# A pixel-transformer block on one core: the cross-attention stretch is planned anew (two join banks, half-step products with U, ternary weights in one step, a shared port in the plan)

## The chip, the core and the metric

The kernel runs on one core of a Trainium2 chip. The core has five engines with a queue of instructions each, which run in order: TensorE (PE, with its weight loads PEld), VectorE (DVE), ScalarE (ACT), GpSimd (POOL) and SyncE (SP), which here only issues DMAs. They meet through semaphores. The metric is the device time of one execution in microseconds, as the median of several runs.

## The reference

Two samples of 1024 tokens with 256 features go through a conditioned transformer block and then a quantised feed-forward layer, all in float32.

```python
h1 = adaln(x, t, norm1_w, norm1_b)              # layernorm(x) * (1 + scale) + shift
x = mha(h1, h1, attn1_wq, attn1_wk, attn1_wv, attn1_wo, attn1_bo) + x
h2 = adaln(x, t, norm2_w, norm2_b)
x = mha(h2, context, attn2_wq, attn2_wk, attn2_wv, attn2_wo, attn2_bo) + x
h3 = adaln(x, t, norm3_w, norm3_b)
x = glu_ff(h3, ff_w1, ff_b1, ff_w2, ff_b2) + x  # a * gelu(gate) @ w2 + b2
...
h = bitlinear(x, w1, b1)     # rmsnorm, rows rounded to 8 bits, weights to -1, 0, 1
h = jax.nn.gelu(h, approximate=False)
return bitlinear(h, w2, b2)
```

Attention has 16 heads of 64; the context has 77 keys for each sample. The ternary weights are `clip(round(w * scale), -1, 1) / scale` with `scale = 1 / mean(|w|)`.

## The kernel before, in words

**Three stretches.** The first runs self-attention in a loop written out by hand (up to about 770 us). The second, from there to about 961 us, is ordered by a planner and holds the end of self-attention, all of cross-attention and the preparation of the ternary weights. The third, also planned, is the gated feed-forward with the quantised layer behind it.

**The planner.** `Plan.add(engine, us, fn, after, rank, ring, behind)` records a step: its engine, how long it is taken to be, what it waits for, its rank among ready steps (a smaller number first), and a ring of PSUM banks that it takes a bank from. `Plan.run` plays the steps through with those durations, always takes the engine that can begin first, and calls each step's function then. That fixes the order of the instructions in the queues of PE, DVE, ACT and POOL. The durations do nothing on the chip. SP's order is made by the framework.

**Self-attention's end.** A unit `u` is a pair of heads with half of the tokens; `LAST` is number 31. Its scores (L425) of eight key blocks are copied by ACT (L1072), DVE keeps a running maximum `macc` (L441), which is folded (L446 to L463), goes through DRAM (`md`, `wide`, L467 and L468) and to a PSUM bank `mb` (L472). DVE subtracts it (L481; POOL for block 5, L477), ACT takes exponentials (L484), POOL adds them up in `pacc` (L491), PE multiplies with V (`pav`, L499, copied out at L515). The sums: PE adds over partitions (`tot`, L522, bank "f"), ACT copies (L532), SP packs them through DRAM (L536, L541), DVE inverts (L544), SP spreads them (`rinv`, L547 and L549), POOL normalises (L555). `back_to_tokens` then multiplies with the output weights in four steps t = 0, 2, 4, 6 (`po`, L360, all in bank "f"), and DVE adds each to the residual `r_sb` (L412), through a list `due` which `settle` empties.

**Cross-attention** works in four batches of 512 tokens. Keys and values are folded into G and U beforehand. For a batch, PE makes five tiles of scores against G (`sc`, L846, two banks in turn); ACT copies each to `p` (L856), DVE keeps the maximum (L862) and halves it (`largest`, L866). PE turns `macc` (a **join**, L873, four 128x128 transposes), DVE folds it to one maximum for each head and row and spreads it (`few`, `wide`, L877 and L883), PE turns it back, and DVE subtracts that row from each `p` (L896). ACT takes exponentials (L901 to L906), POOL sums them (L912, L916). The sums go the same way through PE, DVE (with a reciprocal, L881) and PE; POOL divides two of the tiles by them (L928, from a copy, L920), DVE three (L930). Then four products with U, of ten pieces each (`out`, L937, banks "av" and "f" in turn), which DVE adds to the residual (L949). The joins use two half banks, "A" and "B". Before, a batch's maximum is turned into B and back into A, its sums into A and back into B.

**Norms between.** `half_norm` takes statistics on DVE (L116, L117), begins a root there (L135, L84), steps it on POOL in 14 small instructions (L142 to L147), centres on ACT (L154), turns on PE (`pt_n`, L163) and scales on ACT (L170). It makes the second sample's input of cross-attention and the feed-forward's first input. POOL adds the output bias (L181).

**Ternary weights** w1 and w2, one after the other: SP loads them (`raw`, L1345), ACT takes sums of absolute values (L1363), PE the mean (`pm`, L1374), DVE scales, clips and rounds in two tiles of three operations (L1390, L1388, L1393), PE turns them (`pt_w`, L1407), ACT copies (L1411). Before, w2 is loaded into the tiles of w1 once those are free. `load_ff` loads the feed-forward's weights (L1331, L1333). The third stretch's products are L1799 and L1825.

Of the kernel before, what the change touches and what calls it, by code (L numbers as in the profile page):

```python
# [18 lines left out]
FP = mybir.dt.float32  # L19
# [24 lines left out]
def block_kernel(ctx: ExitStack, tc: tile.TileContext, a: dict, out: bass.AP):  # L44
# [141 lines left out]
    class Plan:  # L186
# [6 lines left out]
        def add(self, engine, us, fn, after=(), rank=0.0, ring=None, behind=()):  # L193

            behind = [s for s in behind if s is not None]
            after = [s for s in after if s is not None] + behind
            self.steps.append((engine, us, fn, after, rank, ring, behind))
            return len(self.steps) - 1  # L200

        def run(self, bufs):
# [6 lines left out]
            end, free = {}, dict.fromkeys(("PE", "ACT", "DVE", "POOL", "SP"), 0.0)  # L209
            left = set(range(len(self.steps)))  # L210

            def ready(s):
# [12 lines left out]
                return max([free[engine]] + [end[a] + l for a, l in zip(need, late)])  # L225

            while left:
# [19 lines left out]
                free[engine], end[s] = t + busy, t + made  # L247
                left.remove(s)
# [12 lines left out]
    with ExitStack() as sa:  # L261
# [137 lines left out]
        def back_to_tokens(b, grp, t):  # L399

            aT = aTs[b, grp]
            po = piece_bank("po")
# [431 lines left out]
        class Batch:  # L834


            def __init__(self, n):
                self.n, self.b, self.at = n, n // 2, n % 2 * 512
                self.sc, self.t = {}, {}
# [92 lines left out]
            def out(self, i, bank):  # L932
                self.po = getattr(self, "po", {})
                po = self.po[i] = bank
                for piece in range(NPIECE):
                    at = piece % 2 * 512 + i * P
                    nc.tensor.matmul(  # L937
                        po[:, :D],
# [5 lines left out]
                if i == 3:  # L944
                    del self.t
# [176 lines left out]
        settle()  # L1122
# [9 lines left out]
        row, sums, steps = {}, {}, {}  # L1132
# [44 lines left out]
        for u in (LAST - 2, LAST - 1, LAST):  # L1177
            s = add("PE", 0.75, lambda u=u: summed(u, piece_bank), [running.get(u)], -55, "f")
# [6 lines left out]
            )  # L1185
        given = []
        for t in range(0, TB, 2):
            u = LAST - 1 + t // 4
            s = add(
                "PE", 1.9, lambda t=t: back_to_tokens(B - 1, NP // 2 - 1, t),  # L1190
                [normal[u], normal[LAST - 2]] + given[-1:], -45 + t, "f",
            )
            given.append(add("DVE", 0.7, settle, [s], -45 + t))


        def half_norm(n, b, half, ready, rank, turn_after=()):
# [5 lines left out]
            s = add("DVE", 0.4, lambda: norm.root_begun(at, 4), s, rank)  # L1202
            s = add("POOL", 2.9, lambda: norm.root_stepped(at, 4), [s], rank)
# [51 lines left out]
        for n, x in enumerate(batches):  # L1255
            r = 10.0 * n
            b, half = n // 2, n % 2
            kept, larger = {}, {}
            for k in range(NTILE):
# [8 lines left out]
                score[n, k] = add("PE", 3.5, lambda x=x, k=k: x.scores(k), waits, r, "s", room)  # L1268
# [11 lines left out]
            s = add("DVE", 0.65, x.largest, [larger[NTILE - 1]], r - 21)  # L1280
# [630 lines left out]
```

## Time and profile before

| | us |
|---|---|
| median of 3 runs | 1180.77 (1179.68 to 1182.17) |
| the profiled execution | 1184.35 |
| its span on the core | 1181.7 |

| stretch, us | PE busy | DVE busy | ACT busy | POOL busy |
|---|---|---|---|---|
| 20 to 770 | 735.92 | 649.98 | 618.53 | 637.95 |
| 770 to 961 | 182.37 | 132.73 | 79.12 | 115.87 |
| 961 to 1181.7 | 211.96 | 144.85 | 109.24 | 84.72 |

The span runs from the first to the last instruction that the profiler recorded; 2.65 us of the profiled execution lie around it. In the rows below, an operation is named by its line, its engine, its output and inputs, its shape, and in brackets the idle time of the engine before it with what ended that. A matmul's end is modelled, so neighbours overlap by some tenths; distances between starts are exact. A float32 product is two records.

### The profile page before, as it was taken

What the parts mean: (1) busy time and instruction counts of PE and PEld (TensorE: products, weight loads), DVE (VectorE), ACT (ScalarE), POOL (GpSimd) and SP (SyncE); (2) the same over time, 40 slices, a digit from 0 to 9 for tenths busy, and PEclk for the clock granted to TensorE, in tenths of its full rate; (3) what the DMA queues carried; (4) which work ended last, traced back from release to release, by engine and by line L of the source; (5) the groups of instructions that cost most, each with busy time, mean ns of one, the idle gap of its engine ahead of it and who ended that gap; (6) DMA issues with size and microseconds to landing.
All of it is one profiled execution on the core that took longest, in us unless ns stands there. A gap on an engine that the chain in (4) does not pass through costs nothing.

```text
span 1181.7 us, 16400 instructions
## 1 busy us (share of the span) xinstructions
PE 1146.3 (97%) x5812; PEld 557.9 (47%) x5812; DVE 936.0 (79%) x1324; ACT 814.7 (69%) x1017; POOL 849.5 (72%) x644
## 2 busy tenths in 40 slices
PE   8998999999999999999999999999899999999997
PEld 4332334334334343343433333346577766486685
DVE  4799789879888988898978988966777733578597
ACT  4788887888887888888789878754633311556366
POOL 5589888888888788889878998877845613433235
PEclk9999999999999999999999999999999999999999
DMA  7111212212121221211113212121102021000000
GB/s 233 37 32 46 79 49 65 71 53 70 46 79 60 62 62 56 74 49 57 52 52 103 72 38 86 55 64 41 45 18 90 1 65 34 1 18 10 10 9 28
DMA packets 65031, 64.15 MB, mean 54 GB/s; under 512 B 23675, under 2 KB 54709, under 8 KB 64309
## 3 DMA queue, kind: packets, MB, share of 16 engines
q1 hardware_dynamic: 64885, 63.10, 17.2%
q8 instruction: 45, 0.74, 0.3%
q14 instruction: 37, 0.30, 0.1%
q10 hardware_dynamic: 64, 0.02, 0.0%
HBM read 55.36 MB, written 7.73 MB: 53 GB/s over the span
## 4 chain that ended last, share of the span: by engine, by line
PE 78%; DVE 14%; ACT 5%; issue 2%; DMA 1%; POOL 1%; SPq 0%; DVEq 0%; ACTq 0%; POOLq 0%
PE sc L425 17%; PE pav L499 16%; PE pp L360 8%; PE pu L1799 8%; PE sc L846 5%; PE pv L360 4%; PE po L1825 4%; DVE macc L441 4%; PE po L937 4%; DVE sT L481 3%; PE po L360 3%; ACT sT L1072 2%; PE tot L522 1%; PE pu L1654 1%; DVE p L896 1%
## 5 line engine op out<-in xcount | busy, mean ns | idle before, releaser
L491 POOL TENSOR_TENSOR pacc<-pacc,sT 128x1024 f32<-128x1024 f32 x192 | 455.6, 2373 | 47.2 <-ACT sT L484 36.7
L1072 ACT COPY sT<-sc 128x1024 f32<-128x1024 f32 x256 | 247.6, 1015 | 55.5 <-PE sc L425 48.8
L441 DVE TENSOR_TENSOR macc<-macc,sc 128x1024 f32<-128x1024 f32 x192 | 233.6, 1217 | 63.0 <-ACT sT L1072 51.7
L484 ACT ACTIVATE sT<-sT 128x1024 f32<-128x1024 f32 x256 | 259.2, 1061 | 11.7 <-DVE sT L481 10.8
L425 PE MATMUL sc<-qT,kT 64*128 64x512 f32 x1024 | 258.0, 619 | 6.4 <-DVE macc L441 5.8
L481 DVE TENSOR_TENSOR sT<-sT,mb 128x1024 f32<-128x1024 f32 x224 | 260.4, 1207 | 2.5 <-ACT mb L472 2.4
L499 PE MATMUL pav<-sT,v 128*64 128x512 f32 x1024 | 249.3, 607 | 4.8 <-ACT sT L484 4.4
L425 PEld LDWEIGHTS sc<-qT,kT 64*128 64x128 f32 x1024 | 85.7, 185 | 146.0 <-DVE macc L441 63.1
L499 PEld LDWEIGHTS pav<-sT,v 128*64 128x64 f32 x1024 | 62.4, 136 | 155.7 <-issue 75.4
L1799 PE MATMUL pu<-h2T,ffw 128*128 128x512 f32 (+1 forms) x320 | 114.4, 509 | 0.1
L491 POOL TENSOR_TENSOR pacc<-sT 128x1024 f32<-128x1024 f32 x32 | 76.2, 2382 | 41.1 <-ACT sT L484 41.1
L1799 PEld LDWEIGHTS pu<-h2T,ffw 128*128 128x128 f32 x320 | 59.6, 190 | 45.4 <-issue 40.4
L477 POOL TENSOR_TENSOR sT<-sT,wide 128x1024 f32<-128x1024 f32 x32 | 76.0, 2375 | 1.7 <-DMA wide<-md 1.7
L846 PE MATMUL sc<-h1T,G 128*128 128x512 f32 x160 | 74.1, 610 | 2.8 <-DVE macc L862 1.7
L937 PE MATMUL po<-U,p 128*128 128x256 f32 x320 | 71.6, 382 | 0.0
L937 PEld LDWEIGHTS po<-U,p 128*128 128x128 f32 x320 | 60.7, 192 | 8.3 <-issue 0.2
L360 PE MATMUL pp<-h1T,wk 128*64 128x512 f32 x256 | 62.2, 607 | 0.9 <-ACT h1T L617 0.9
L360 PE MATMUL po<-wo,aT 128*64 128x256 f32 x512 | 61.1, 380 | 0.2 <-POOL aT L555 0.2
L360 PE MATMUL pv<-wv,h1T 128*64 128x256 f32 x512 | 60.8, 379 | 0.0
L360 PE MATMUL pp<-h1T,wq 128*64 128x512 f32 x256 | 60.5, 593 | 0.0
L1817 DVE SCALAR_TENSOR_TENSOR gT<-pu,vecT,ge 128x512 f32<-128x512 f32 (+1 forms) x40 | 25.6, 641 | 43.4 <-ACT ge L1810 38.7
L846 PEld LDWEIGHTS sc<-h1T,G 128*128 128x128 f32 x160 | 47.2, 304 | 26.0 <-DVE macc L862 4.1
(195 smaller groups left out, 1481.5 us busy)
## 6 DMA issues: line engine op xcount, KB each, us to landing
wide<-md SPq DMA_DIRECT2D x32, 512.0 KB
rinv<-td SPq DMA_DIRECT2D x64, 128.0 KB
ffw<-in_L_xcond_ff_w_dram SPq DMA_DIRECT2D x3, 1024.0 KB
gd<-cw SPq DMA_DIRECT2D x32, 80.0 KB
ud<-cw SPq DMA_DIRECT2D x32, 80.0 KB
U<-ud SPq DMA_DIRECT2D x2, 1280.0 KB
wk<-in_L_xcond_attn_wk_dram SPq DMA_DIRECT2D x16, 128.0 KB
wq<-in_L_xcond_attn_wq_dram SPq DMA_DIRECT2D x16, 128.0 KB
```

Of the source, the lines that this page charges most:

```text
L360: nc.tensor.matmul(dst[half, :], lhsT=lhsT[:, half], rhs=rhs, start=start, stop=stop)
L425: nc.tensor.matmul(sc[:, j * 512 : (j + 1) * 512], lhsT=kTs[b, pair][rows, kb * P : (kb + 1) * P], rhs=qTs[b, pair][rows, qh * 512 : (qh + ...
L441: nc.vector.tensor_tensor(maccs[u], old, sc, ALU.max)
L477: nc.gpsimd.tensor_tensor(t, t, wides[u], ALU.subtract)
L481: nc.vector.tensor_tensor(sT[u, kb], sT[u, kb], mbs[u], ALU.subtract)
L484: nc.scalar.activation(sT[u, kb], sT[u, kb], AF.Exp)
L491: nc.gpsimd.tensor_tensor(paccs[u], old, sT[u, kb], ALU.add)
L499: nc.tensor.matmul(pavs[u][j * DH : (j + 1) * DH, :], lhsT=vs[b, pair // 2][:, kb, at : at + DH], rhs=sT[u, kb][:, j * 512 : (j + 1) * 512 ...
L846: nc.tensor.matmul(sc[:, j * 512 : (j + 1) * 512], lhsT=Gs[self.b][c][:, 2 * k + j, :], rhs=hT[:, c, self.at : self.at + 512], start=(c == 0),
L937: nc.tensor.matmul(po[:, :D], lhsT=self.t[piece // 2][:, at : at + P], rhs=Us[self.b][:, piece, :], start=(piece == 0), stop=(piece == NPI ...
L1072: nc.scalar.copy(sT[v, kb], sc)
L1799: nc.tensor.matmul(pu[:, k * 512 : k * 512 + n], lhsT=ffw1[c][:, at : at + P], rhs=hT[:, c, at0 : at0 + n], start=(c == 0), stop=(c == DC ...
```

## The change

All edits lie in the planner and in the second stretch.

- `Plan.add` takes `port`: in the plan such a DVE step begins when POOL's running step is over, and POOL counts as taken while it runs. It is set for the begin of the root and for the ternary steps. `Plan.run` takes times at which engines become free.
- The last `settle` of the loop becomes a step; `tot` stands behind it. `back_to_tokens` of the last group takes the banks "av" and "f" in turn, and each addition is a step of its own.
- A batch's maximum uses bank A both ways, its sums bank B.
- A product with U is two steps of five pieces; a step of no length takes its bank.
- For each half of a ternary weight the three DVE operations are one step. w2 gets space of its own (a tile of the tag "aT") and is loaded with w1; the feed-forward's weights wait for the last scores alone.
- Ranks and durations of many steps are new.

```diff
-        def add(self, engine, us, fn, after=(), rank=0.0, ring=None, behind=()):
+        def add(self, engine, us, fn, after=(), rank=0.0, ring=None, behind=(), port=False):
...
+            free.update(begin)
...
                 late = (wait * (self.steps[a][0] != engine) for a in need)
-                return max([free[engine]] + [end[a] + l for a, l in zip(need, late)])
+                port = [free["POOL"]] if self.steps[s][7] else []
+                return max([free[engine]] + port + [end[a] + l for a, l in zip(need, late)])
...
+                if self.steps[s][7]:
+                    free["POOL"] = t + busy
                 left.remove(s)
...
             aT = aTs[b, grp]
-            po = piece_bank("po")
+            po = po or piece_bank("po")
...
-            def out(self, i, bank):
-                self.po = getattr(self, "po", {})
-                po = self.po[i] = bank
-                for piece in range(NPIECE):
+            def out(self, i, half):
+                for piece in range(half * NTILE, (half + 1) * NTILE):
                     at = piece % 2 * 512 + i * P
                     nc.tensor.matmul(
-                        po[:, :D],
+                        self.po[i][:, :D],
                         lhsT=self.t[piece // 2][:, at : at + P],
                         rhs=Us[self.b][:, piece, :],
                         start=(piece == 0),
                         stop=(piece == NPIECE - 1),
                     )
-                if i == 3:
+                if i == 3 and half:
...
-        settle()
...
-        row, sums, steps = {}, {}, {}
+        row, sums = {}, {}
+        settled = add("DVE", 0.7, settle, [], -90)
...
-            s = add("PE", 0.75, lambda u=u: summed(u, piece_bank), [running.get(u)], -55, "f")
+            s = add("PE", 0.75, lambda u=u: summed(u, piece_bank), [running.get(u)], -55, "f", [settled])
...
             )
+        def either_bank(i):
+            return psx.tile([P, 512], FP, tag="f" if i % 2 else "av", name="po")
         given = []
         for t in range(0, TB, 2):
             u = LAST - 1 + t // 4
             s = add(
-                "PE", 1.9, lambda t=t: back_to_tokens(B - 1, NP // 2 - 1, t),
-                [normal[u], normal[LAST - 2]] + given[-1:], -45 + t, "f",
-            )
-            given.append(add("DVE", 0.7, settle, [s], -45 + t))
+                "PE", 1.9, lambda t=t: back_to_tokens(
+                    B - 1, NP // 2 - 1, t, either_bank(t // 2)
+                ),
+                [normal[u], normal[LAST - 2]], -45 + t, "f" if t // 2 % 2 else "av",
+                [evac[LAST]],
+            )
+            given.append(add("DVE", 0.7, lambda: due.pop(0)(), [s], -45 + t, None, given[-1:]))
...
-            s = add("DVE", 0.4, lambda: norm.root_begun(at, 4), s, rank)
-            s = add("POOL", 2.9, lambda: norm.root_stepped(at, 4), [s], rank)
+            s = add("DVE", 0.4, lambda: norm.root_begun(at, 4), s, rank, port=True)
+            s = add("POOL", 4.0, lambda: norm.root_stepped(at, 4), [s], rank)
...
-                score[n, k] = add("PE", 3.5, lambda x=x, k=k: x.scores(k), waits, r, "s", room)
+                score[n, k] = add("PE", 3.55, lambda x=x, k=k: x.scores(k), waits, r, "s", room)
                 order.append(score[n, k])
...
-                "PE", 0.6, lambda x=x: x.turned(bank(1), x.macc), [s, joint], -70, "B"
+                "PE", 0.6, lambda x=x: x.turned(bank(0), x.macc), [s, joint], -70, "A"
             )
             s = add("DVE", 1.2, lambda x=x: x.folded(ALU.max), [s], r - 21)
             up = add("PE", 0.6, lambda x=x: x.turned(bank(0)), [s, joint], -70, "A")
             run = None
             exps = {}
             for k in range(NTILE):
-                s = add("DVE", 1.22, lambda x=x, k=k: x.shifted(k), [up, kept[k]], r - 19)
+                s = add("DVE", 1.22, lambda x=x, k=k: x.shifted(k), [up, kept[k]], r - 9)
...
-            s = add("POOL", 1.3, x.total, [run], r - 1)
+            s = add("POOL", 1.6, x.total, [run], r - 1)
             s = tot_done[n + 2] = add(
-                "PE", 0.6, lambda x=x: x.turned(bank(0), x.pacc), [s], -70, "A"
-            )
-            s = add("DVE", 1.4, lambda x=x: x.folded(ALU.add), [s], r - 21)
+                "PE", 0.6, lambda x=x: x.turned(bank(1), x.pacc), [s], -70, "B"
+            )
+            s = add("DVE", 1.75, lambda x=x: x.folded(ALU.add), [s], r - 21)
             up = add("PE", 0.6, lambda x=x: x.turned(bank(1)), [s], -70, "B")
...
-                def job(x=x, i=i):
-                    x.out(i, piece_bank("po2") if i % 2 else psx.tile([P, 512], FP, tag="av", name="po2"))
-                s = add(
-                    "PE", 4.75, job, parts + [loaded.get((b, "u"))], 50 + r,
+                def begin(x=x, i=i):
+                    x.po[i] = either_bank(i)
+                first = add(
+                    "PE", 0.0, begin, parts + [loaded.get((b, "u"))], 40 + r,
                     "f" if i % 2 else "av", outs[n][-1:] + [evac[LAST]],
                 )
+                s = first
+                for half in range(2):
+                    s = add(
+                        "PE", 2.2, lambda x=x, i=i, half=half: x.out(i, half), [first, s], 40 + r
+                    )
                 outs[n].append(s)
-                sums[n].append(add("DVE", 0.42, lambda x=x, i=i: x.added(i), [s], r - 15))
+                sums[n].append(add("DVE", 0.42, lambda x=x, i=i: x.added(i), [first, s], r - 15))
...
         def load_raw(name):
-            raws[name] = []
-            for i in range(2):
-                t = p2.tile([P, 1024], FP, tag="kT", name="raw")
-                raws[name].append(t)
+            if name == "w1":
+                raws[name] = [p2.tile([P, 1024], FP, tag="kT", name="raw") for _ in range(2)]
+            else:
+                t = w8.tile([P, 2 * S], FP, tag="aT", name="raw")
+                raws[name] = [t[:, :1024], t[:, 1024:]]
+            for i, t in enumerate(raws[name]):
...
-        raw_in = {"w1": add("SP", (1.0, 8.0), lambda: load_raw("w1"), [loaded[1, "u"]], 80)}
-        add("SP", (1.2, 15.0), load_ff, [raw_in["w1"]], 80, None, order)
+        raw_in = {
+            name: add("SP", (1.0, 8.0), lambda name=name: load_raw(name), [], 80, None,
+                      given + [loaded[1, "u"]])
+            for name in ("w1", "w2")
+        }
+        add("SP", (1.2, 15.0), load_ff, [], 80, None, order)
...
-        last = []
         for name in ("w1", "w2"):
-            if name == "w2":
-                raw_in["w2"] = add("SP", (1.0, 8.0), lambda: load_raw("w2"), last, 80)
...
             s = add("DVE", 0.25, lambda name=name: ternary_total(name), s, 80)
-            s = add("PE", 0.4, lambda name=name: ternary_mean(name), [s], 40, "s")
+            s = add("PE", 0.4, lambda name=name: ternary_mean(name), [s], 65, "s")
             s = add("DVE", 0.4, lambda name=name: ternary_scale(name), [s], 80)
             last = []
             for i in range(2):
-                u = add("DVE", 1.27, lambda name=name, i=i: ternary_clip(name, i, False), [s], 80)
-                u = add("DVE", 1.17, lambda name=name, i=i: ternary_clip(name, i, True), [u], 80)
-                last.append(add("DVE", 0.95, lambda name=name, i=i: ternary_round(name, i), [u], 80))
-            s = add("PE", 1.1, lambda name=name: ternary_turned(name), last, 45, "s")
+                for job in (
+                    lambda name=name, i=i: ternary_clip(name, i, False),
+                    lambda name=name, i=i: ternary_clip(name, i, True),
+                    lambda name=name, i=i: ternary_round(name, i),
+                ):
+                    s = add("DVE", 0.75, job, [s], 80, port=True)
+                last.append(s)
+            s = add("PE", 1.1, lambda name=name: ternary_turned(name), last, 65, "s")
...
-            half_norm(2, 0, half, sums[half], 40, [order[-1], *outs[half]])
+            half_norm(2, 0, half, sums[half], 55, [order[-1], *outs[half]])
-        plan.run({"s": 2, "f": 1, "av": 1, "A": 1, "B": 1})
+        plan.run({"s": 2, "f": 1, "av": 1, "A": 1, "B": 1}, DVE=1.2, ACT=0.7, POOL=5.1)
```

## The prediction

> **What bounds the kernel now.** I read the page's busy table first, then the waits of the TensorE, then its timeline from 750 us on, where the changed steps run, then that stretch's windows for the granted clock, then the other engines' timelines there.
>
> ```profile
> PE 1146.3 (97%) x5812; PEld 557.9 (47%) x5812; DVE 936.0 (79%) x1324; ACT 814.7 (69%) x1017; POOL 849.5 (72%) x644
> ...
> PE pt_w L1407 <- DVE wq L1393: 2.9, 1, 2.9
> PE tot L522 <- DVE r_sb L412: 2.1, 1, 2.1
> PE sc L846 <- DVE macc L862: 1.7, 1, 1.7
> ```
>
> PE is 97% busy, and the change takes no product away. So only idle PE can be saved, and the waits name three of its longest gaps: all three end on a DVE instruction, all three lie in the stretch that the plan orders. What a gap costs is seen in the timeline:
>
> ```profile
> 766.43 1.90 PE L360 MATMUL po<-wo,aT 128*64 128x256 f32 x16
> 770.38 1.08 PE L522 MATMUL tot<-pacc,ones 128*32 128x256 f32 x8 [2.06 <-DVE r_sb L412]
> 771.39 3.11 PE L499 MATMUL pav<-sT,v 128*64 128x512 f32 x8
> ...
> 927.44 0.22 PE L1407 MATMUL pt_w<-ident_bf,wq 128*128 128x128 bf16 x1
> 930.57 1.60 PE L1407 MATMUL pt_w<-ident_bf,wq 128*128 128x128 bf16 x15 [2.91 <-DVE wq L1393]
> 931.96 1.06 PE L873 MATMUL join<-ident,pacc 128*128 128x128 f32 x4
> 932.81 5.18 PE L937 MATMUL po<-U,p 128*128 128x256 f32 x20
> ...
> 771.40:774.40 3.00, 3.00 (x12) 0.76 (x8) 3.00 (x3) 2.84 (x4) 2.92 (x2) 0.60 0.54 190
> 931.00:934.00 3.00, 3.00 (x18) 2.82 (x17) 1.89 (x6) 1.80 (x1) 2.10 (x11) 0.50 0.00 0
> ```
>
> Columns of the last two: window, its length, busy time (count) of PE, PEld, DVE, ACT, POOL, then the clock, DMA share, GB/s. After gaps of 2.06 and 2.91 us the clock is 0.60 and 0.50, and the work behind them runs slow (pav 3.11 us; elsewhere 1.94).
>
> Gap lengths therefore undercount. I measure each loss from start to start, with undisturbed rows: scores of a tile 3.6 us (3.74 when another kind follows), a product with U 4.32, pav 1.8, po 1.88, tot 0.57, four transposes 0.44, eight 0.88, ternary turn 0.89.
> - A, 768 us: po starts at 766.43, so tot could at 768.25, and scores at 770.6. They start at 774.43: **3.8**.
> - B, 827.9 to 844.1: 16.2 us hold 11.0 of work (two po, four joins, one score, two norm turns): **5.2**. It is a heap of waits of 0.2 to 0.9.
> - C, 892: scores due at 892.2 start at 894.05: **1.9**.
> - D, 927: from 927.44 to the products at 939.14 are 11.7 us with 7.0 of work: **4.7**.
> - One product at 867.2 takes 0.3 too long.
>
> Sum 15.9 us. That is the most the change can bring.
>
> *A rule and the rows.* The Trainium skill, "TensorE: Matmul & The Clock Gate", Part 1, says the clock halves after at least one idle window of about 3.4 us. By it A and D, shorter, would cost their idle alone, 2.1 + 2.9, and the sum would be about 12.4. The clocks above say otherwise, and I take the rows. It cuts both ways: a new gap over 2 us costs some 1.7 us more.
>
> **The change, part by part.** No matmul, DVE, ACT or POOL operation is added or removed; durations in the plan only steer the order. I followed the built order of the changed kernel on each engine (no time stands in it) with the rows above, DVE 1.22 (1.14 in a run), ACT copies 1.0 and exponentials 1.06, POOL sums 2.4 (2.47 with the gaps).
>
> *1. Settling as a step; tokens go back through two banks (A).* tot waited for bank "f", which DVE freed late (L412). Now pav, which needs only exponentials done at 769.1, and the first scores come first; tot starts at 773.8, long after 770.2. A goes. Behind it LAST-2's sums reach ACT at 774.8, not 771.6, its queue being full of exponentials; their DMA reload stands behind the maximum's send at 777.3. So rinv lands about 784; POOL uses it at 785.5 anyway. Cost 0.
>
> *2. Self-attention's end and batch 0.* From 768.25 in the new order: pav 770.05, scores 773.8, tot 774.35, two pav 777.95, two scores 785.15, tot 785.7, two scores 792.9. LAST's shifts run on DVE from 786.4 to 794.4, exponentials to 796.3, so its four pav (792.9 to 800.0) wait for none. In the trace before, the same work ended at 804.2.
> SP: G's second load now stands ahead of rinv for LAST-1. It waits for the last pav (800.0). Its transfer took about 2.4 us, rinv's about 1.6; rinv lands near 806.5, in time if POOL is busy until then. POOL sums LAST from 789.9, 7 × 2.47 = 17.2, to 807.1, and about 1.2 more for two DVE operations that take its port: 808.3. PE, at 808.1, waits **0.3**; the normalising (1.28) ends at 809.7 and the first po waits **0.7**.
>
> *3. Batch 1 and the end of the tokens (B).* po, po, scores k=2 and 3 carry PE to 820.75. The normalising of LAST now stands on POOL behind batch 0's sums (809.7 to 819.5) and the 14 root instructions. DVE's begin of the root takes the port and ends near 820.1; so the maximum of k=2 ends at 821.3, and scores k=4 wait **0.7**. Root 4.1 us, to 824.2, normalising to 825.5: po t=4 waits **0.6**. Then total 826.8, joins, norm turn, po, and the inverse's join at 831.2 against PE's 831.15: **0.05**. The heap B becomes these 2.35 us.
>
> *4. Joins: macc and maxima in bank A, both sums in B.* Same 32 transposes. Before, bank B was shared by macc of the next batch and the sums' row, so a macc had to wait for the divisions. From 831 on I find each join ready before PE (batch 1's sums end at 855, used at 859; batch 3's macc at 895.4, used at 895.7).
>
> *5. Half steps.* 16 × 10 products remain; a join may enter after five, 2.2 us in. PE pays no extra instruction; other banks are written in between. Gain: no join waits for a whole 4.3.
>
> *6. Ternary weights (C, D).* Before, these DVE operations ran beside POOL:
>
> ```profile
> 890.13 2.73 DVE L1393 TENSOR_SCALAR wq<-raw 128x1024 bf16<-128x1024 f32 x1
> 913.30 0.69 DVE L1393 TENSOR_SCALAR wq<-raw 128x1024 bf16<-128x1024 f32 x1
> 804.76 2.47 DVE L866 TENSOR_TENSOR macc<-macc 128x512 f32<-128x512 f32 x1
> 830.30 0.69 DVE L866 TENSOR_TENSOR macc<-macc 128x512 f32<-128x512 f32 x1
> ```
>
> The first delayed scores at C, its like delayed D. In the new order all 12 stand at the end, after POOL's last division. For w1: 0.9 for the scales, 6 × 0.7 = 4.2, ready 5.3 after the mean; PE arrives after 1½ products, 6.5. For w2: 5.1 us behind the add of the next product, ready 1.2 us before PE. Cover 1.2 us in both; if POOL's two divisions still run, up to 4.7 us shows. ACT's two copies (1.84) end before the feed-forward needs their banks.
> w2's raw load (1 MB, two issues for one: 0.4 us on SP) takes the place of ffw2's (1 MB, 768.4), so td and md behind it move by 0.4, inside the POOL cover. ffw2 and ffw1 load after the last scores (889), 55 us before use, where before ffw1 was issued at 897.
>
> *The rule against this change.* The Trainium skill, "SBUF — State Buffer", "SBUF: two separate sides": DVE and GpSimd share a port pair, locked for a whole instruction, for DVE operations of two SBUF inputs too. L866 above agrees: 2.47 beside POOL, 0.69 without. But the plan marks only root begin and ternary; "largest" (L866) is costed 0.7 unmarked. By the plan, joins cost 0; by the rule three of four largest wait up to 1.8, 5.4 us in all. In my order batch 0's and 3's lie under PE's own work; batch 1's ends as PE arrives. I keep 0, and 5.4 for the range.
>
> *Sum.* After 831.65 PE has 115.0 us of work, so the products end at 946.7 instead of 960.7: 14.0. By the other sum 15.9 − 2.35 = 13.5. One more near miss (scores of batch 3, k=3, maximum ready 0.2 us ahead) and the wear of many waits: 1. **12.5 us**. The feed-forward stage has the same order, and its first loads are released by the last product with U, so it moves as a whole. Span 1181.7 − 12.5 = 1169.2; 2.65 us lie around it in the profiled execution (1184.35). Runs without a profile had the median 1180.77, so **1168**.
>
> **Rivals.**
> - *Waits come back in part*: the unmarked port uses (5.4) or the ternary cover gone (4.7), one with its slow clock (1.7). Gain about 6: 1174. For: margins of 0.2 to 1.2 us at six places. Against: PE gets slack back at the products, 4.3 each.
> - *Given back later*: the feed-forward's end (1160 to 1181, PE 13.5 of 21 busy) hangs on something that doesn't move. Then 1181. Against: no load there is timed by anything but the release.
> - *Slower*: LAST's normalising, the only link through two DMA round trips, two DVE instructions behind po adds, and now POOL's root. po t=4 is next in PE's order, so each us late is one of PE. It decides from 13 us late (825.5 becomes 839), beyond 1181; at 17 late, with the slow clock, 1186. For: four queues in one chain, G and the root newly ahead. Against: rinv should land near 821, and the part before it moves little.
> - *The change doesn't do what it says* in one point: the port is only planned, nothing reserves it; that is in the first rival.
>
> **How the numbers follow.** Forecast 0.65 (own range 1165 to 1171), partly back 0.22 (1171 to 1178), given back 0.06, slower 0.07. About 0.2% (2.4 us) can be told from no change, so faster is below 1178.4: 0.87, same 0.06, slower 0.07. The range goes from the whole 15.9 us (1164.9) to a gain of 3.3 (1177.5) and leaves out some 0.16.
>
> **What will show it.** Right: no gap at tot L522 and clock 1.00 around 768; last pav near 800; no wait of pt_w on wq; ternary operations 0.7 each; products end near 947; PE busy as before but for the slow-clock work. Wrong: a PE gap over 2 us between 800 and 835, L871 at 2.4 us with a join waiting, or ternary at 2.7.

## The result, and the profile after

| | before | after |
|---|---|---|
| median, us | 1181.07 (1179.68 to 1182.17, 4 runs) | 1170.71 (1168.51 to 1171.38, 4 runs) |
| profiled execution, its span | 1184.35, 1181.7 | 1170.28, 1168.5 |

The ratio is 0.9908 (95% interval 0.9891 to 0.9924): 10.4 us faster, 2.7 us short of the forecast. Five more runs of the changed kernel in a later comparison gave 1170.10 (0.9903, interval 0.9888 to 0.9917); the nine together have the median 1170.28, which is the figure "after" below.

The page of the changed kernel, its first row:

```profile
PE 1139.9 (98%) x5812; PEld 555.7 (48%) x5812; DVE 926.2 (79%) x1324; ACT 814.8 (70%) x1017; POOL 847.3 (73%) x644
```

The work is the same (the counts have not moved). PE's busy time fell by 6.4 us. About half of that, 3.4 us, is matmuls that no longer run at a reduced clock: in the profile before, two stretches of 3.41 us behind gaps A and D ran at a clock of 0.50 (from 770.38 and from 930.80 us), and the profile after has none there. The other half is not traced further; the ends of matmuls are modelled.

TensorE's timeline of the changed kernel (start, duration, line, operation, idle before and what ended it):

```profile
766.02 1.90 PE L365 MATMUL po<-wo,aT 128*64 128x256 f32 x16
767.82 2.02 PE L504 MATMUL pav<-sT,v 128*64 128x512 f32 x8
769.78 3.81 PE L851 MATMUL sc<-h1T,G 128*128 128x512 f32 x8
773.52 0.64 PE L527 MATMUL tot<-pacc,ones 128*32 128x256 f32 x8
...
808.98 0.64 PE L527 MATMUL tot<-pacc,ones 128*32 128x256 f32 x8 [1.18 <-POOL pacc L496]
...
830.74 0.66 PE L878 MATMUL join<-ident,wide 128*128 128x128 f32 x4 [0.53 <-DVE few L882]
...
835.35 0.63 PE L878 MATMUL join<-ident,wide 128*128 128x128 f32 x4 [0.41 <-DVE p L935]
...
865.81 0.63 PE L878 MATMUL join<-ident,wide 128*128 128x128 f32 x4 [1.06 <-DVE p L935]
...
934.92 1.06 PE L1427 MATMUL pt_w<-ident_bf,wq 128*128 128x128 bf16 x16
...
940.18 1.06 PE L1427 MATMUL pt_w<-ident_bf,wq 128*128 128x128 bf16 x16
...
947.61 2.74 PE L1820 MATMUL pu<-h2T,ffw 128*128 128x512 f32 x6
```

The gap before tot is gone, and both ternary turns start without one. From the loop's last `po` to the first product of the feed-forward (called the stretch below) are 947.61 − 766.02 = 181.6 us; before, 960.72 − 766.43 = 194.3. The difference, 12.7, is what two profiled executions show. The first product in TensorE's timeline before:

```profile
960.72 31.38 PE L1799 MATMUL pu<-h2T,ffw 128*128 128x512 f32 x72
```

The feed-forward moved as a whole: 1168.5 − 947.6 = 220.9 us, and 221.0 before. Windows of the changed kernel (columns as in the prediction) show the clock at 1.00, and 3.9 us without PE work between 770 and 948 us, where before the 191 us from 770 to 961 held 8.6:

```profile
771.40:774.40 3.00, 3.00 (x16) 1.45 (x16) 2.97 (x3) 2.85 (x4) 2.92 (x2) 1.00 0.26 108
...
770.00:948.00 178.00, 174.11 (x749) 128.31 (x750) 122.79 (x186) 78.98 (x99) 113.38 (x105) 1.00 0.12 42
```

VectorE's timeline of the changed kernel, one halved maximum and a ternary operation:

```profile
797.68 1.64 DVE L871 TENSOR_TENSOR macc<-macc 128x512 f32<-128x512 f32 x1
...
930.70 0.69 DVE L1413 TENSOR_SCALAR wq<-raw 128x1024 bf16<-128x1024 f32 x1
```

All twelve ternary operations take 0.69 to 0.75 us. The four halved maxima take 1.64, 1.28, 0.69 and 1.25: POOL is at work during the three longer ones.

### The profile page after: what moved, and what is told of

It is laid out like the page before. It is cut to its first block, busy times and chain, and to the rows that moved or that the text cites. A ratio compares the mean times of both kernels' runs of the same rounds, so it can differ in the third digit from the quotient of the medians.

```text
span 1168.5 us, 16402 instructions
## 1 busy us (share of the span) xinstructions
PE 1139.9 (98%) x5812; PEld 555.7 (48%) x5812; DVE 926.2 (79%) x1324; ACT 814.8 (70%) x1017; POOL 847.3 (73%) x644
## 4 chain that ended last, share of the span: by engine, by line
PE 80%; DVE 11%; ACT 5%; issue 1%; POOL 1%; DMA 1%; DVEq 0%; ACTq 0%; POOLq 0%
PE sc L430 17%; PE pav L504 16%; PE pu L1820 9%; PE pp L365 8%; PE po L940 6%; PE pv L365 4%; PE sc L851 4%; PE po L1846 4%; PE po L365 4%; DVE macc L446 4%; DVE sT L486 3%; ACT sT L1075 2%; PE tot L527 1%; ACT sT L489 1%; PE pu L1675 1%
## 5 line engine op out<-in xcount | busy, mean ns | idle before, releaser
L1846 PE MATMUL po<-ffw,gT 128*128 128x256 f32 x256 | 57.3, 379 | 0.0
```

The lines of the kernel that those rows point to most:

```text
L1846: nc.tensor.matmul(po[:, :D], lhsT=self.gT[:, f, k * P : (k + 1) * P], rhs=ffw2[:, f, :], start=(f == 0), stop=(f == FS - 1),)
```

## The experiments

Times are medians; each ratio is to the kernel before in the same comparison (1180.5 us for e1 to e4, 1181.3 for e5 to e8, 1181.7 for e9 to e12).

### Which part makes the gain: one part at a time on the kernel before

**e1**: only the end of self-attention (settled step, two banks, additions as steps).

```diff
-        settle()
...
+        settled = add("DVE", 0.7, settle, [], -90)
...
-                "PE", 1.9, lambda t=t: back_to_tokens(B - 1, NP // 2 - 1, t),
-                [normal[u], normal[LAST - 2]] + given[-1:], -45 + t, "f",
...
+                "PE", 1.9, lambda t=t: back_to_tokens(
+                    B - 1, NP // 2 - 1, t, either_bank(t // 2)
+                ),
+                [normal[u], normal[LAST - 2]], -45 + t, "f" if t // 2 % 2 else "av",
+                [evac[LAST]],
```

> The kernel before with only the first part: the loop's last settling is a planned step, tot stands behind it, and the last tokens go back through two banks. Theory (each part repairs the gap that the prediction gave it): the gap of 2.06 us at tot near 768 us is gone, the clock there is 1.00 instead of 0.60, the gaps at 892 and 927 stay, and the gain is the 3.8 us of A, perhaps 1 or 2 of B: 1176 to 1178. Rival (only the whole new order helps, a part alone lets the next wait take its place): no gain, 1180 to 1182.

Measured: 1179.77, ratio 0.9991 (0.9979 to 1.0003), not to be told from no change. TensorE's timeline of e1:

```profile
766.66 2.02 PE L499 MATMUL pav<-sT,v 128*64 128x512 f32 x8
768.81 0.64 PE L522 MATMUL tot<-pacc,ones 128*32 128x256 f32 x8
...
928.49 1.01 PE L1413 MATMUL pt_w<-ident_bf,wq 128*128 128x128 bf16 x15 [2.91 <-DVE wq L1399]
...
939.50 1.13 PE L937 MATMUL po<-U,p 128*128 128x256 f32 x4 [1.39 <-POOL p L928]
941.80 16.67 PE L937 MATMUL po<-U,p 128*128 128x256 f32 x76 [1.18 <-POOL p L928]
```

Gap A is gone, gap D is not, and the planner has put products in front of POOL's divisions. The local gain was spent inside the same stretch.

**e2**: only the ternary weights (one step of three operations, marked, w2 in its own place).

```diff
-            s = add("PE", 0.4, lambda name=name: ternary_mean(name), [s], 40, "s")
+            s = add("PE", 0.4, lambda name=name: ternary_mean(name), [s], 65, "s")
...
+                    s = add("DVE", 0.75, job, [s], 80, port=True)
```

> The kernel before with only the ternary part: three DVE operations in one step, w2's raw load in a place of its own, begin with POOL's port in the plan. Theory: the ternary operations of the DVE take 0.7 us each instead of up to 2.7, the waits of 1.7 us (scores at 892) and 2.9 us (turn at 930) are gone; gain 6.6 us less what comes back, 1175 to 1177; the gap at 768 stays at 2.06. Rival: the ternary work is only moved and delays the shifts or the maxima of other batches; gain under 2 us.

Measured: 1184.90, ratio 1.0034 (1.0025 to 1.0044), slower. TensorE's timeline of e2, and below it its windows:

```profile
769.54 0.64 PE L525 MATMUL tot<-pacc,ones 128*32 128x256 f32 x8 [2.06 <-DVE r_sb L415]
...
933.63 1.06 PE L1416 MATMUL pt_w<-ident_bf,wq 128*128 128x128 bf16 x16
...
940.99 2.07 PE L940 MATMUL po<-U,p 128*128 128x256 f32 x4 [3.57 <-POOL p L931]
```

```profile
770.00:774.00 4.00, 4.00 (x17) 2.01 (x14) 3.96 (x5) 3.45 (x4) 3.92 (x2) 1.00 0.49 193
938.00:942.00 4.00, 1.01 (x2) 0.84 (x3) 2.35 (x2) 3.62 (x4) 3.42 (x2) 0.72 0.00 0
```

The turns wait for nothing, and a new gap of 3.57 us stands behind a division. The first window answers a second question: the gap at tot is 2.06 us as in the kernel before, and this time the clock behind it is 1.00.

**e3**: only the join banks (a batch's maximum in A both ways, its sums in B).

```diff
-                "PE", 0.6, lambda x=x: x.turned(bank(1), x.macc), [s, joint], -70, "B"
+                "PE", 0.6, lambda x=x: x.turned(bank(0), x.macc), [s, joint], -70, "A"
...
-                "PE", 0.6, lambda x=x: x.turned(bank(0), x.pacc), [s], -70, "A"
+                "PE", 0.6, lambda x=x: x.turned(bank(1), x.pacc), [s], -70, "B"
```

> The kernel before with only the banks of the joins exchanged: maxima in A both ways, sums in B both ways. Theory (the heap of waits from 828 to 844 us comes from several causes, of which the shared bank is one): some tenths of the 5.2 us there, gain 0 to 1.5, 1179.5 to 1181. Rival (the two banks are the heart of the change): that heap falls to under 2 us and the gain is 3 us or more, under 1178.

Measured: 1177.19, ratio 0.9971 (0.9961 to 0.9982): 3.3 us faster, though it made a gap of its own. TensorE's timeline of e3:

```profile
837.03 1.11 PE L873 MATMUL join<-ident,wide 128*128 128x128 f32 x4 [3.71 <-DVE p L896]
```

That join takes 1.11 us where others take 0.6: the clock from 837 to 841 is 0.50. The two ternary turns fall at 902.44 and 921.09 in e3 and wait for nothing; the edit touches neither. So the gain came by way of the order, not from these turns.

The three parts together would give 0.7 − 4.4 + 3.3 = −0.4 us if they added up. All of the change gives 10.4, and what is in it beside these three (half steps, new numbers) is worth 3.2 and 4.6 by e6 and e10 below, which does not fill the difference. **The parts are not additive.**

### What a gap of 2 to 3 us costs

**e4**: the kernel before, with 14 transposes of the identity, read by nobody, in the gap at 768.

```diff
+        fill = two_banks("fill")
+        for i in range(14):
+            nc.tensor.transpose(fill[:, i % 4 * P : (i % 4 + 1) * P], ident, ident)
         settle()
```

> The kernel before with 14 transposes of the unit matrix (float32, 128x128, 1.5 us by the joins' 0.44 for four) put into PE's queue ahead of tot, that is into the gap at 768 us; their output is read by nobody. Theory (the gap costs more than its 2.06 us because the clock falls behind it): tot still starts near 770.4, but the clock between 771 and 774 us stays near 1.00, pav takes 1.9 us instead of 3.1, and the scores start some 1.6 us earlier; gain about 1.6 us. Rival (the slow pav has another cause, for instance its wait for exponentials): pav still takes 3.1 us, and nothing is gained.

Measured: 1180.53, ratio 0.9995 (0.9983 to 1.0007): no gain. TensorE's timeline of e4, and its window behind the gap at 928.80:

```profile
766.27 1.90 PE L360 MATMUL po<-wo,aT 128*64 128x256 f32 x16
...
768.20 1.75 PE L1124 MATMUL fill<-ident 128*128 128x128 f32 x14
770.22 0.64 PE L522 MATMUL tot<-pacc,ones 128*32 128x256 f32 x8 [0.27 <-DVE r_sb L412]
...
928.80 1.01 PE L1410 MATMUL pt_w<-ident_bf,wq 128*128 128x128 bf16 x15 [2.91 <-DVE wq L1396]
...
957.31 1.88 PE L1802 MATMUL pu<-h2T,ffw 128*128 128x512 f32 x4
```

```profile
931.00:934.00 3.00, 3.00 (x16) 2.64 (x15) 0.98 (x2) 1.96 (x4) 1.30 (x6) 1.00 0.01 3
```

The gap of 2.91 us is there, unfilled, and the clock behind it is 1.00; in the kernel before's profile the same gap was followed by 0.50. So a slowed clock behind such a gap belongs to some executions and not to others, and filling the gap can save its slow clock only where there was one.

Which executions, the traces show. Between the first and the last microseconds of a span, the clock falls to 0.50 for 3.41 us at a time (6.83 once each in e2 and e3). Where a trace has several such stretches, their starts lie whole multiples of 3.4133 us apart: before, at 12.62, 770.38 and 930.80, which are 222 and then 47 times that. So in these traces the clock changes on a grid of slots of 3.41 us, and a slot doesn't begin where a gap begins. What goes with the slow clock is how little PE work the slot with the gap in it has left. Windows over single slots of the kernel before (gap A, the slot behind it, gap D):

```profile
766.97:770.38 3.41, 1.35 (x14) 0.64 (x11) 3.31 (x5) 3.10 (x4) 3.33 (x2) 1.00 0.53 165
770.38:773.79 3.41, 3.41 (x14) 0.97 (x16) 3.41 (x4) 2.23 (x4) 3.25 (x3) 0.50 0.76 263
927.39:930.80 3.41, 0.50 (x7) 0.24 (x5) 3.41 (x4) 0.00 (x0) 3.25 (x4) 1.00 0.00 0
```

The same of e2 (the slot with the larger part of gap A), and below it of e4 (with the larger part of gap D):

```profile
765.69:769.10 3.41, 1.79 (x18) 0.90 (x14) 3.31 (x4) 3.41 (x4) 3.19 (x2) 1.00 0.58 153
```

```profile
926.93:930.34 3.41, 1.54 (x21) 1.52 (x22) 3.30 (x9) 0.49 (x1) 2.92 (x8) 1.00 0.00 0
```

Where the gap of 2.06 us fell into one slot, it left it 1.35 us of work, and the next slot is slow; where the edge of a slot cut it in two, 1.79 are left, and the next is not slow. With the gap of 2.91 us it is 0.50 (slow) and 1.54 (not). From 760 to 962 us in the 14 profiles, the slow clock sets in eight times, each time behind a slot with 0.50 to 1.58 us of PE work; where it doesn't set in, the slot before has 1.54 or more. The limit seen here is thus near 1.55 us. It isn't the whole rule: in e7 the clock is slow from 1152.99, in the feed-forward, behind a slot with 1.95 us of work.

What a slow slot costs is seen in e4. Its stretch has none and takes 957.31 − 766.27 = 191.0 us; the kernel before's has two and takes 194.3. At half the clock two slots of 3.41 lose 3.4 us of work, and 3.3 is the difference. (The filling itself costs nothing: `tot` starts 3.95 us behind the loop's last `po` in both.) So without a slow clock the change gains 191.0 − 181.6 = 9.4 us.

The results list the mean clock of each run; 49 runs of the kernel before from the comparisons with experiments, by that clock:

| mean clock of the run | runs | mean time, us |
|---|---|---|
| 1.000 | 4 | 1179.4 |
| 0.999 | 11 | 1180.4 |
| 0.998 | 12 | 1180.2 |
| 0.997 | 13 | 1181.8 |
| 0.996 | 3 | 1182.8 |
| 0.995 | 6 | 1183.2 |

One slow slot takes 1.7 us from PE and some 0.0014 from the mean clock, so these are runs with none, one (0.999 and 0.998), two (0.997) and up to three; slow time in the last microseconds of the span is counted too and blurs the rows. The profiled execution (1184.35) was of the last row. The nine runs of the changed kernel have clocks of 0.998 or 0.999; in the two that were profiled the one slow slot lies at the start, from 12 to 16 us, where the kernel before's profile has one too. Like with like, the 23 runs of the kernel before at 0.998 or 0.999 have the mean 1180.3, and the nine 1170.2: 10.1 us. The first row (9.1 above the nine) has one slow slot less than they, the last (13.0 above) about two more.

### What each part is worth within the whole change

**e5**: the changed kernel with the join banks as before (the diff of e3 backwards).

> The changed kernel with one part undone: macc is turned into bank B again and the sums into A first, as before. Theory (the planner's order is what counts, and it needs the free bank to place batch work early; the exchange alone gained 3.3 us): some 3 us of the gain are lost, 1172.5 to 1175. Rival (in the new order the joins have slack enough, so the banks don't matter any more): 1170 to 1171.5.

Measured: 1167.94, ratio 0.9888 (0.9873 to 0.9903). The exchange of the banks, worth 3.3 us alone, is worth nothing here. In the profile it costs 1.1 us: e5's stretch takes 944.77 − 764.25 = 180.5. The medians are 2.3 us apart (the intervals overlap), but all four runs of e5 have a mean clock of 1.000, so they lack the slow slot that each of the nine has.

**e6**: the changed kernel with a product's ten pieces in one step.

```diff
-                for half in range(2):
-                    s = add(
-                        "PE", 2.2, lambda x=x, i=i, half=half: x.out(i, half), [first, s], 40 + r
-                    )
+                s = add(
+                    "PE", 4.4, lambda x=x, i=i: (x.out(i, 0), x.out(i, 1)), [first, s], 40 + r
+                )
```

> The changed kernel with the products with U as whole steps of ten pieces. Theory (a join that stands behind a whole product comes up to 2.2 us later, but two of four joins in the changed trace waited for DVE right behind a half product anyway): 0 to 2 us slower, 1170.5 to 1173. Rival (half steps carry the gain of the product stretch): over 3 us slower, above 1173.5.

Measured: 1173.45, ratio 0.9937 (0.9920 to 0.9954), 3.2 us above the changed kernel; its interval doesn't meet that of the five later runs, but overlaps that of the first four, which ends at 0.9924. TensorE's timeline of e6:

```profile
926.07 0.38 PE L1393 MATMUL pm<-wpart,ones 128*128 128x1 f32 x2 [1.42 <-ACT h2T L170]
...
929.09 9.45 PE L940 MATMUL po<-U,p 128*128 128x256 f32 x36 [1.18 <-POOL p L933]
```

With coarser steps the planner puts the mean and a product where their inputs are late. The stretch takes 948.86 − 764.58 = 184.3 us, 2.7 more than the changed kernel's, and 1.7 of that is a slow slot that follows these gaps (clock 0.50 from 928.58 to 931.99).

**e7**: the changed kernel, the plan blind to the port.

```diff
-                port = [free["POOL"]] if self.steps[s][7] else []
+                port = []
...
-                if self.steps[s][7]:
-                    free["POOL"] = t + busy
```

> The changed kernel with a plan that doesn't know of the shared port; ranks and durations stay. Theory (POOL's load sets the length of the ternary operations only where they stand beside it): if the planner leaves them behind the last division, nothing changes, 1170 to 1171.5, and the operations take 0.7 us each. Rival (the port in the plan is what put them there): some of them stand beside POOL's sums again and take up to 2.7 us, PE waits for a turn, 1173 or more.

Measured: 1168.70, ratio 0.9897 (0.9883 to 0.9912), and the same 181.6 us for the stretch. The ternary operations still stand at the end and take 0.69 to 0.75 us. The mark is worth nothing that can be measured; what moved them is the rest of the plan.

**e8**: the changed kernel, with the two join halves as two tiles of one bank each in place of two halves of one tile.

```diff
...
-            banks["m"] = psx.tile([P, 1024], FP, tag="mb", name="join")
+            mb_stack.close()
+            psj = sa.enter_context(tc.tile_pool(name="psj", bufs=1, space=PSUM))
+            for k in range(2):
+                banks[k] = psj.tile([P, 512], FP, tag=f"j{k}", name="join")
...
-            return banks["m"][:, k * 512 : (k + 1) * 512]
+            return banks[k]
```

> The changed kernel with two PSUM tiles of one bank for the joins instead of one tile of two banks; same order of work. Theory (the two gaps of 0.41 and 1.06 us before the maxima's second joins come from DVE's divisions and ACT's copy that read the other bank of the same tile, so they are no true waits): both gaps go and 1.5 us with them, 1168.5 to 1169.7. Rival (those joins wait for something that they need): the gaps stay, 1170 to 1171.

Measured: 1167.01 (1165.53 to 1167.94), ratio 0.9880 (0.9865 to 0.9895), 3.3 us below the changed kernel. All five engines have the same instructions in the same order in both. TensorE's timeline of e8, with the counterparts of the joins at 830.74, 835.35 and 865.81 above:

```profile
764.33 1.90 PE L367 MATMUL po<-wo,aT 128*64 128x256 f32 x16
...
828.51 0.65 PE L880 MATMUL join<-ident,wide 128*128 128x128 f32 x4
...
832.55 0.60 PE L880 MATMUL join<-ident,wide 128*128 128x128 f32 x4
...
861.21 0.60 PE L880 MATMUL join<-ident,wide 128*128 128x128 f32 x4
...
942.97 3.60 PE L1825 MATMUL pu<-h2T,ffw 128*128 128x512 f32 x8
```

None waits. With the order the same, only the waits can differ: a join into one half was held until VectorE had read the *other* half of the tile. VectorE's timeline of the changed kernel shows it for the join at 830.74:

```profile
829.66 0.43 DVE L888 COPY wide<-few 128x512 f32<-128x512 f32 x1
830.00 0.69 DVE L882 TENSOR_REDUCE few<-join 128x64 f32<-128x512 f32 x1
```

That join turns the sums' `wide` into half B. Its input is ready at 830.09, yet it starts when VectorE has read half A for the maxima, at 830.69. The brackets come from semaphores, so this is a wait that the program was given, for its one tile, and not one that the chip imposed.

The stretch falls from 181.6 to 942.97 − 764.33 = 178.6 us, 3.0 less. Before the stretch e8's profile is ahead by another 1.7 us, which fits that it has no slow slot at the start; two of the four runs have a mean clock of 1.000.

### Structure, numbers, and a better kernel

**e9**: the changed kernel unaltered.

> The changed kernel unaltered, so that e5, e7 and e8 can be set against more runs of it and the three variants below beside it on one chip. Theory (the slow clock behind the gaps of before is paid in some executions only, 12 to 13 us is what the profiled execution shows and about 10.4 the ordinary one): 1170.0 to 1171.5, ratio 0.991. Rival (the first measurement of it fell low or high by chance): outside of that, 1168 (the whole forecast) or 1173.

Measured: 1170.10, as told with the result; every gap of its profile in the stretch is where the first had it (1.18 at tot, 0.53, 0.40, 0.34, 1.06 at the joins).

**e10**: the change's structure with the ranks, durations and begin times of before.

```diff
-                s = add("DVE", 1.22, lambda x=x, k=k: x.shifted(k), [up, kept[k]], r - 9)
+                s = add("DVE", 1.22, lambda x=x, k=k: x.shifted(k), [up, kept[k]], r - 19)
...
-            s = add("PE", 1.1, lambda name=name: ternary_turned(name), last, 65, "s")
+            s = add("PE", 1.1, lambda name=name: ternary_turned(name), last, 45, "s")
...
-        plan.run({"s": 2, "f": 1, "av": 1, "A": 1, "B": 1}, DVE=1.2, ACT=0.7, POOL=5.1)
+        plan.run({"s": 2, "f": 1, "av": 1, "A": 1, "B": 1})
```

> The changed kernel's structure (settled step, two banks for the tokens, joins exchanged, half steps, ternary in one step, w2 in its own place) with the ranks, durations and begin times of before, and the root unmarked. Theory of the structure (the gain lies in what the steps may do, and the plan's numbers are a touch-up): at most 3 us lost, 1170 to 1174, no gap over 2 us in PE's row between 766 and 950. Theory of the order (single parts gave 0.7, -4.1 and 3.4 us, so the numbers that set the order make most of it): 1175 or more, with waits of PE on POOL's divisions (L928, L931) and on ternary steps between products as in the single parts.

Measured: 1174.66, ratio 0.9945 (0.9933 to 0.9958), between the two theories: 7.0 us of the gain come with the structure, 4.6 (to e9 beside it) with the numbers. VectorE's timeline of e10 and then TensorE's:

```profile
910.33 2.69 DVE L1410 TENSOR_SCALAR raw<-raw,winv 128x1024 f32<-128x1024 f32 x1
...
915.81 2.73 DVE L1413 TENSOR_SCALAR wq<-raw 128x1024 bf16<-128x1024 f32 x1
```

```profile
822.37 3.81 PE L851 MATMUL sc<-h1T,G 128*128 128x512 f32 x8 [1.39 <-DVE macc L867]
...
830.65 0.66 PE L878 MATMUL join<-ident,macc 128*128 128x128 f32 x4 [1.35 <-DVE macc L871]
...
849.24 2.93 PE L940 MATMUL po<-U,p 128*128 128x256 f32 x6 [1.20 <-POOL p L933]
```

The ternary steps stand beside POOL again, at 2.7 us, marked or not: nobody waits for them there. The loss lies mostly between 820 and 852, in these gaps of about 1.3 us and, in this profile, a slow slot behind the last of them (clock 0.50 from 848.97 to 852.38).

**e11**: e8 with the banks of e5.

> The changed kernel with two join tiles of one bank each, and with a batch's maximum in B and back in A, its sums in A and back in B, as before. If the two effects add up (e8 gave 3.7 us, e5 2.8 us against the changed kernel's 1170.7): 1164 to 1165. If e5 gained only because its order met fewer of the false waits between the two halves of one tile, splitting leaves it nothing: 1167 to 1168, like e8. If the order falls badly: 1170 or more.

Measured: 1168.34, ratio 0.9887 (0.9872 to 0.9902). The effects don't add up: splitting leaves e5's order nothing. In e5's profile no join waits for VectorE, so there was no such false wait to remove.

**e12**: e8, with the port marked for the halved maximum and the folds too.

```diff
-            s = add("DVE", 0.7, x.largest, [larger[NTILE - 1]], r - 21)
+            s = add("DVE", 0.7, x.largest, [larger[NTILE - 1]], r - 21, port=True)
...
-            s = add("DVE", 1.2, lambda x=x: x.folded(ALU.max), [s], r - 21)
+            s = add("DVE", 1.2, lambda x=x: x.folded(ALU.max), [s], r - 21, port=True)
...
```

> Two join tiles of one bank each, and the port marked in the plan also for the halved maximum (L866 of before) and the folds, which the changed kernel leaves unmarked. If a truer plan gives a better order: 1164 to 1166, with the halved maximum at 0.7 us in all four batches and no join waiting on it. If the marks only tell the plan what costs PE nothing (in the changed kernel three of four halved maxima took 1.25 to 1.64 and no join waited): within 1.5 us of e8's 1167.0, either way. If steps held back for the port come late on VectorE: 1169 or more, with scores waiting on the maximum.

Measured: 1175.81, ratio 0.9950 (0.9937 to 0.9962), 8.8 us above e8. VectorE's groups of e12 between 760 and 960, and TensorE's timeline:

```profile
L873 DVE TENSOR_TENSOR macc<-macc 128x512 f32<-128x512 f32 x4 | 6.9, 1725 | 0.1
```

```profile
822.79 1.10 PE L163 MATMUL pt_n<-ident,xn 128*128 128x128 f32 x8 [1.42 <-ACT p L863]
...
851.39 3.79 PE L853 MATMUL sc<-h1T,G 128*128 128x512 f32 x8 [1.16 <-DVE macc L869]
...
931.51 7.50 PE L942 MATMUL po<-U,p 128*128 128x256 f32 x26 [1.18 <-POOL p L935]
```

The marks did not even get the four halved maxima free of POOL: they take 1.73 us on average, and a join waits 0.6 us for one. A place kept free in the plan was not free on the chip. What the marks did is move the order, for the worse.

The fastest kernel is e8, 14.3 us below the kernel before.

## Why the prediction was right, and where it was off

**The direction and the mechanism** were right: forecast 1168, measured 1170.7, at the upper end of its own range of 1165 to 1171 for the likeliest case. Of its signs, the gap at tot went, the clock around 768 is 1.00, the last of LAST's four pav ended at 799.6 (800 forecast), no turn waits for wq, the ternary operations take 0.7, and the products end at 947.6 (946.7).

**The term that was mis-sized: the slow clock**, in the step "The clocks above say otherwise, and I take the rows". It put gaps A and D at their length plus the slow work behind them, 3.8 and 4.7, and so the whole at 15.9. The rows were true of the execution that was profiled, in which each of the two gaps fell into one slot of the clock. e2, e3 and e4 show the same gaps of 2.06 and 2.91 us without a slow clock behind them. By the rule of the Trainium skill, "TensorE: Matmul & The Clock Gate", Part 1 (a clock halves after an idle window of about 3.4 us), which the prediction set against the rows, the sum was 12.4, less its own losses of 3.35 is 9.1. Measured without a slow slot in the stretch it is 9.4 (191.0 in e4 against 181.6), and with the two slow slots of the profiled execution 12.7. The measured 10.4 lies between, because the ordinary run pays the slow clock in part. The rule is not the whole truth either: none of these gaps is 3.4 us long, and where enough of one fell into a single slot the clock did halve (0.50 before, 0.52 from 930 to 933 in e1). The prediction had both times before it, the profiled execution's and the median 3.6 us below, and took 12.5 off each. It should have read the 3.6 as part of what it was about to count.

**Step 4, "I find each join ready before PE"**, failed at four places: joins waited 0.53 at 830.74, 0.41 at 835.35, 0.34 at 861.93 and 1.06 at 865.81, 2.3 us in all. It took the two banks for independent; e8 shows that they were not while they were halves of one tile. That the sum hardly suffered is in part luck: against these stood the 1 us set aside for near misses and "the wear of many waits", while the waits of steps 2 and 3 came to 1.4 us (1.18 at tot, 0.26 at po t=4) where 2.3 were forecast. Together the gaps of the new stretch are 3.8 us, against 3.35.

**The other steps.** 1 and 2: as forecast, but that the wait for POOL's sums fell on tot as one of 1.18 where 0.3 and 0.7 stood. 3: scores k=4 waited for nothing (0.7 forecast), because the root began at 815.9, not near 820; po t=4 waited 0.26 (0.6). 5: half steps are worth some 3 us within the whole (e6), over half of it slow clock, which the prediction had not put into its sum apart. 6: both turns ready in time, as forecast, and neither the move of w2's load nor of the feed-forward's weights shows in PE's row. Two small slips in its sums (7 × 2.47 is 17.3, not 17.2; 0.9 + 4.2 is 5.1, not 5.3) change nothing.

**The rule on the shared port** (the Trainium skill, "SBUF — State Buffer", "SBUF: two separate sides") agrees with the trace: three of four halved maxima were stretched beside POOL, 2.1 us in all of the 5.4 kept for the range. No gap of PE ends on them. Taking 0 for the time was right, and e12 shows that a plan which keeps the rule at more steps can be worse.

**Open.** Why the order of e5 gives no less than that of the changed kernel, and how the 7 us of e10 divide over the parts of the structure, was not tried. Nor do the runs show what places the slots of the clock against the program, which differs from one execution to the next, or why the feed-forward of e7 met a slow slot behind 1.95 us of work.

## What to carry to other kernels

Before you count a gap's slow clock as gain, set the profiled execution beside the median: what it lies above it was perhaps the very thing that you are counting, and other runs don't pay it. Count the slow slots of each profile and compare like with like. With a list planner, judge an edit by the whole order it makes: parts that gave 0.7, −4.4 and 3.3 us alone gave 10 together, and marking two more kinds of step for the shared port lost 9. And don't let two chains share one PSUM tile, even in separate banks, without looking for waits on the other half: splitting it gave 3 us here with not one instruction moved.

## What the runs showed of the hardware

- The granted clock was 0.50 for 3.41 us at a time (6.83 in e2 and e3), in slots that start whole multiples of 3.4133 us apart within a trace. From 760 to 962 us the slow clock set in behind slots with 0.50 to 1.58 us of PE work (eight times), and never behind one with more; the least without it was 1.54 (e4). So a gap of 2.06 or of 2.91 us slowed the clock in some executions and not in others.
- Two slow slots cost 3.3 us (the stretch of the kernel before and of e4, 194.3 and 191.0).
- A halved maximum (128x512, two SBUF inputs) takes 0.66 to 0.69 us with POOL idle or between its operations and up to 2.77 beside it (e12, 851.28), a ternary operation 0.69 and 2.73. In the changed kernel no gap of PE ends on either.
